# A two-layer sequence kernel on one core: the second layer's input slabs in a range of SBUF of their own, loads placed behind fetches of the last feed-forward, and three orders placed anew

## The chip, the core and the metric

One core of a Trainium2 chip runs the whole program. The metric is the device time of one execution in microseconds, as the median of several runs. TensorE (PE) does the matmuls, VectorE (DVE) and ScalarE (ACT) the elementwise work, GpSimd (POOL) small operations and the stores' DMA issues, SyncE (SP) most loads. All data are float32.

## The reference, cut to what matters

The input x is (4, 512, 128, 64): batch b, time t, features f, channels h. Layer 0:

```
xn = layernorm(x);  k, v = xn@Wk, xn@Wv;  r = sigmoid(xn@Wr)
s_t = decay*s_(t-1) + k_t*v_t;            x = x + (r*s) @ Wo
x = x + gelu(conv over f of layernorm(x))
x = x + layernorm(causal depthwise conv over t, 3 taps, of layernorm(x))
x = x + gelu(x @ ffn_W1 + b1) @ ffn_W2 + b2
```

Layer 1:

```
trend = moving_average(x, 25 steps of t);  seasonal = x - trend
xs = rfft(seasonal, over t)[:, :128]
out = trend + irfft(einsum('bmnc,cmk->bknc', xs, w_real + i*w_imag))
```

## The kernel before

Layer 0 handles each of the four sequences (b = 0 to 3) in stages: `project` (J: key, value and gate matmuls), `scan` (Z: the recurrence and a norm's moments), `attend_and_convolve` (A), `convolve_time` (C), `open_feed` (O: the first two units' input) and `feed_forward` (F). A unit is a pair of 128-row chunks by 512 time steps; `NPR` = 32 units make a sequence. Each stage is a Python generator that traces some work and yields a weight.

PE's order is written out: under `manual_schedule` PE's instructions run as traced, and `in_turn` walks two streams of stages side by side, a step of the one or of the other by how far each has come. The yield `CHAIN` (6.0) ends a step of a dependent chain, so that the other stream is stepped next:

```python
((0, (O, 0.05), (F, 0.95)), (2, (J, 0.88), (Z, 0.12))),
((1, (C, 1.0)), (2, (A, 1.0))),
((1, (O, 0.05), (F, 0.95)), (3, (J, 0.88), (Z, 0.12))),
((2, (C, 1.0)), (3, (A, 1.0))),
((2, (O, 0.05), (F, 0.95)), (3, (C, 0.95), (O, 0.05))),
((3, (F, 1.0)), (3, (nothing, 1.0))),
```

So sequence 3's feed-forward runs alone at the end of layer 0. The other engines and queues are ordered by a planner at compile time, which issues what is ready by its own estimate, in order of tracing where several are. Three calls bind it: `keep_in_program_order(i)` puts an instruction behind the one traced before it on its engine; `issue_after(i)` puts what is traced in its block, on the engine of i, behind i (the order only, no wait for the end of i). Waits for data and for a place in SBUF are added by the framework.

SBUF is given out in pools, one behind the other, and a pool that is opened later over the range of closed ones waits for them as a whole. Layer 0 has `decay` (2,048 bytes per partition), `fr` (tags `x1`, `z`, `xp`, `wx`, `wo`, `wcs`), `const`, `bk` and more; layer 1 begins again at the start with `dft` (2,048 bytes), `io` (tag `big`, five buffers of 8,192 bytes for slabs and mixing weights, and smaller tiles), `const1` and `spec` (the spectrum `xf`).

`wx` holds the projections' weights, the scan's `kv`, and in the last two feed-forwards the units' results, which DVE writes (L759) and PE transposes (L765) before they are copied to `ob` (L773, L778) and stored to `x4` in DRAM. In a feed-forward `residual` fetches `kx` and `kh` (L607) for the unit two ahead, DVE works on them (L692, L693, L704), PE makes `widen` (L733), ACT the activation `mid` (L738), and PE `narrow` (L746).

`project` for b > 1 loads weights for two units at a time and scales them on DVE (L358) before PE reads them (L408). The spread of a column over all rows (`spread`, L242) begins `rows`, whose input `rs` comes from POOL (L234) after DVE's copy of the moments (L269) and a few tiny operations (to L278).

Layer 1 loads a slab (512 time steps by 512 columns, 1 MB, three DMAs at L938 to L940) and `transform` makes `v`, `u` and `ev` of it on DVE (L959, L960, L963), `edge` copies on ACT (L956), and a group of two slabs' matmuls on PE (L971, L979, L988), copied to `xf` by ACT (L995). Sixteen groups make a pair of sequences. Then come `mix` (L1013, L1017) and `invert` (L1039 to L1073).

Of the kernel before, what the change touches and what calls it, by code (L numbers as in the profile page):

```python
# [1 line left out]

# [1 line left out]

# [6 lines left out]
F32 = mybir.dt.float32  # L11
AF = mybir.ActivationFunctionType
ALU = mybir.AluOpType
# [3 lines left out]
P = 128  # L17
# [28 lines left out]
@with_exitstack  # L46
def conv_seq_kernel(
    ctx: ExitStack,
    tc: tile.TileContext,
    x: bass.AP,  # L50
    xt: bass.AP,
    vecs: bass.AP,
    wkvr: bass.AP,
    wo: bass.AP,
    wdec: bass.AP,
    wconv: bass.AP,
    fbias: bass.AP,
    w1: bass.AP,
    fb1: bass.AP,
    w2: bass.AP,  # L60
    fb2: bass.AP,
    wri: bass.AP,
    dftv: bass.AP,
    dftd: bass.AP,
    dfte: bass.AP,
    idfte: bass.AP,
    idfto: bass.AP,
    avg: bass.AP,
    avgh: bass.AP,
    out: bass.AP,  # L70
):
    B = x.shape[0]
    dram = ctx.enter_context(tc.tile_pool(name="dram", bufs=1, space=DRAM))
    x4 = [dram.tile([T, D], F32, tag=f"x4_{b}", name=f"x4_{b}") for b in range(B)]

    layer0(tc, dram, x, xt, vecs, wkvr, wo, wdec, wconv, fbias, w1, fb1, w2, fb2, x4)
    layer1(tc, x4, wri, dftv, dftd, dfte, idfte, idfto, avg, avgh, out)


@with_exitstack  # L80
def layer0(ctx, tc, dram, x, xt, vecs, wkvr, wo, wdec, wconv, fbias, w1, fb1, w2, fb2, x4):
# [10 lines left out]

    decay = ctx.enter_context(tc.tile_pool(name="decay", bufs=1))
    fr = ctx.enter_context(tc.tile_pool(name="fr", bufs=3))
    const = ctx.enter_context(tc.tile_pool(name="const", bufs=1))
    bk = ctx.enter_context(tc.tile_pool(name="bk", bufs=2))
    rowp = ctx.enter_context(tc.tile_pool(name="rowp", bufs=1))
# [49 lines left out]
    nc.vector.tensor_copy(decb, dec.to_broadcast([P, T]))  # L147


    cgr = const.tile([P, NPR, H], F32, name="cgr")  # L150

    at_one = const.tile([P, 2], F32, name="at_one")
    nc.vector.tensor_reduce(at_one[:, 0:1], ident.rearrange("p (q k) -> p q k", k=32)[:, :, 1], mybir.AxisListType.X, ALU.add)
# [142 lines left out]
        return xp  # L296

    def spare(tag, n):
        return fr.tile([P, 2, n], F32, tag=tag, name=tag, bufs={"z": 4, "wx": 2}.get(tag, 3))

    def c_bank():
        return two(ps_c, "c")
# [17 lines left out]
    held = [False]  # L320
    narrowly = set()
    unscanned = [True]


    def project(b):
# [36 lines left out]
        ws, xps, xks = {}, {}, {}  # L362
        if b > 1:
            weights(0)
            for k in range(2):
                scale_weights(k, ws[k], True)
            xps[0] = load_x(b, 0)
        for i in range(NPR):
            first, last = i == 0, i == NPR - 1
# [51 lines left out]
    def scan(b):  # L421
# [13 lines left out]
        if b == 0:  # L435
# [25 lines left out]
            nc.vector.tensor_copy(qo[S:P, 0:S], pq[S:P, 0:S])  # L461
            nc.vector.tensor_scalar_mul(qo[S:P, S:], pq[S:P, S + 2 :], 1.0 / D)
        gw, bw, qo = sums["gw"], sums["bw"], sums["qo"]
        rb, mb = yield from rows(bank, rs, mean, "rm" if b > 1 else "rm3")
        if b == 0:
            kv = two(fr, "x1")
# [49 lines left out]
    def attend_and_convolve(b):  # L516
# [29 lines left out]
        def convolve(i):  # L546
            cv = c_bank() if i % 2 or held[0] else two(ps_m, "m")
            for h in range(2):
                for j in range(2):
                    q = 32 * (2 * h + j)  # L550
                    nc.tensor.matmul(
                        cv[h * H : (h + 1) * H, j, :], lhsT=cgr[q : q + 2, i, :], rhs=mb[q : q + 2, :],
                        start=True, stop=False,
                    )
            for j in range(2):
                c = 2 * i + j
                for n, h in neighbours(i % 2, c):
                    if 0 <= n < NCH:
                        rs = halves[rows_of(n // 2 % 2, n - c)]
                        nc.tensor.matmul(  # L560
                            cv[halves[h], j, :], lhsT=ws[n][rs, P:], rhs=zs[n][rs, :], start=False, stop=False
                        )
            for j in range(2):
                c = 2 * i + j
                nc.tensor.matmul(cv[:, j, :], lhsT=ws[c][:, 0:P], rhs=zs[c], start=False, stop=True)
            nc.scalar.activation(cv, cv, AF.Gelu_apprx_tanh)
            x2 = two(bk, "x2")
            nc.vector.tensor_tensor(x2, cv, x1s.pop(i), ALU.add)  # L568
            nc.gpsimd.dma_start(x2d[b][2 * i : 2 * i + 2].rearrange("c p t -> p c t"), x2)  # L569
            sq2 = bk.tile([P, 2, SL], F32, tag="sq", name="sq2")  # L570
            nc.scalar.activation(sq2, x2, AF.Square)  # L571
            for c in (2 * i - 2, 2 * i - 1):
                zs.pop(c, None)
                ws.pop(c, None)
            if i + 2 < NPR:
                scaled(i + 2)
            waiting[i] = x2, sq2
# [26 lines left out]

    def fetch(tag, src, b, i):
        t = bk.tile([P, 2, SL], F32, tag=tag, name=tag, bufs=3 if tag == "kx" else 2)
        nc.sync.dma_start(t, src[b][2 * i : 2 * i + 2].rearrange("c p t -> p c t"))  # L607
        return t


# [36 lines left out]
    def convolve_time(b):  # L647
        bank = of_a if b == B - 1 else of_p
        made = AHEAD if b in ahead else 0
        moment = carried.pop(b)  # L650
        if made:
            rb, mb = ahead.pop(b)
        else:
            rb, mb = yield from rows(bank, *moment, "rm" if b == B - 1 else "rm3")
        st = bank()
        waiting, added = [], 0
        n = NPR - made
        for k in range(n + 2):
            while waiting and waiting[0][0] == k - 2:
                add_up(st, 0, *waiting.pop(0)[1:], added == 0, added == NPR - 1)  # L660
                added += 1
            if k < n:
                if b == B - 1:

                    x2, xr, to, sq = spare("xp", SL), spare("x1", SL), spare("z", SL), two(bk, "sq")
                else:
                    x2 = bk.tile([P, 2, SL], F32, tag="kx", name="x2", bufs=3)
                    xr, to = two(bk, "kd"), bk.tile([P, 2, SL], F32, tag="k3", name="to", bufs=3)
                    sq = bk.tile([P, 2, SL], F32, tag="sq4", name="sq4", bufs=2)

                normed(b, made + k, x2, xr, rb, mb, made > 0 and k < 4)
                tapped(b, made + k, xr, to)
                nc.scalar.activation(sq, to, AF.Square)
                waiting.append((k, to, sq))
                i = k * made // n
                if i != (k + 1) * made // n:

                    to = fetch("kh", tod, b, i)
                    sq = bk.tile([P, 2, SL], F32, tag="mid", name="sq5", bufs=4)
                    nc.scalar.activation(sq, to, AF.Square)  # L680
                    waiting.append((k, to, sq))
            yield 7.0 * (NPR + 2) / (n + 2)
        mean, sq = yield from finish(st, bank, 4)
        causal[b] = moments(mean, sq, 4)


    def residual(b, i):
# [27 lines left out]
    def feed_forward(b):  # L715
# [69 lines left out]
        for i in range(NPR + lag):  # L785
            if i >= lag:
                store(i - lag)
            for q in range(4):
                done += quarter
                if i < NPR:  # L790
# [3 lines left out]
                        widen(i + 1, q - 2)  # L794
                    if i + 2 < NPR and q == 1:
                        coming = residual(b, i + 2)
                    if i + 2 < NPR and q == 3:
                        x3s[i + 2] = add_residual(b, i + 2, *coming)
                    narrow(i, q)
# [62 lines left out]
    with tc.manual_schedule(engines={nc.tensor.engine}):  # L862
        for _ in project(0):
# [10 lines left out]
            ((2, (O, 0.05), (F, 0.95)), (3, (C, 0.95), (O, 0.05))),  # L874
            ((3, (F, 1.0)), (3, (nothing, 1.0))),
        )


@with_exitstack
def layer1(ctx, tc, x4, wri, dftv, dftd, dfte, idfte, idfto, avg, avgh, out):  # L880

# [7 lines left out]
    G = 2  # L891

    dft = ctx.enter_context(tc.tile_pool(name="dft", bufs=1))
    io = ctx.enter_context(tc.tile_pool(name="io", bufs=2))
    const = ctx.enter_context(tc.tile_pool(name="const1", bufs=1))
    spec = ctx.enter_context(tc.tile_pool(name="spec", bufs=1))
# [29 lines left out]
            nc.vector.tensor_copy(dst, src)  # L926

    def slab(b, s):
        xin = io.tile([P, NT, SL], F32, tag="big", name="xin", bufs=5)
        nc.sync.dma_start(  # L930
            xin, x4[b][:, s * SL : (s + 1) * SL].rearrange("(c p) d -> p c d", p=P)
        )
        return xin

    def shifted_slab(b, s):
        xin = io.tile([P, NT, SL], F32, tag="big", name="xin", bufs=5)
        c = slice(s * SL, (s + 1) * SL)
        nc.sync.dma_start(xin[TURN:P, 0, :], x4[b][0 : P - TURN, c])  # L938
        nc.sync.dma_start(xin[0:TURN, 0, :], x4[b][T - TURN : T, c])
# [3 lines left out]
    def transform(b, xf):  # L943

        for g in range(NS // 2):
            edge = io.tile([P, SL], F32, tag="edge", name="edge")
            uv, ev, pf = [], [], []
            for k in range(2):
                s = 2 * g + k
                c = slice(s * SL, (s + 1) * SL)  # L950
                xin = shifted_slab(b, s)
                ends = xin[0 : 2 * TURN, 0, :]
                if k == 0:
                    first = ends
                for q in (32,) if k == 0 else (H, H + 32):
                    nc.scalar.copy(edge[q : q + 2 * TURN, :], ends)  # L956
                u = io.tile([P, 2, SL], F32, tag="uv0", name="u")
                v = io.tile([P, 2, SL], F32, tag="uv1", name="v")
                nc.vector.tensor_tensor(v, xin[:, 0:2, :], xin[:, 2:4, :], ALU.subtract)  # L959
                nc.vector.tensor_tensor(u, xin[:, 0:2, :], xin[:, 2:4, :], ALU.add)  # L960
                t = io.tile([P, 2, SL], F32, tag="ev", name="ev")
# [35 lines left out]
    def mix(xf):  # L997

        xc = xf.rearrange("p b r (a c l) -> p b r a c l", c=H, l=2)
        for g in range(H // CG):  # L1000

            w = io.tile([P, CG, 2, 2, M], F32, tag="big", name="w", bufs=5)
            nc.sync.dma_start(w, wri[:, g * CG : (g + 1) * CG, :, :, :])
            w4 = w[:, :, 1, 0, :].rearrange("p c (n i m) -> p c n i m", n=2, i=2)[:, :, :, 0, :]
            for t in (w4, w[:, :, 1, 1, 0:H]):
# [23 lines left out]
    def invert(b, xf):  # L1029
# [3 lines left out]
        def waves(s):  # L1033
# [12 lines left out]
            for i, op in enumerate((ALU.add, ALU.subtract)):  # L1046
                nc.vector.tensor_tensor(even[:, i, :], ev[0], two, op)
            for i in range(2):
                pm = io.tile([P, 2, SL], F32, tag=f"uv{i}", name="pm")
                for k, op in enumerate((ALU.add, ALU.subtract)):  # L1050
                    nc.vector.tensor_tensor(pm[:, k, :], even[:, i, :], od[i], op)
                halves[s].append(pm)
# [1 line left out]
        def trends(s):  # L1054
            c = slice(s * SL, (s + 1) * SL)
            xin = slab(b, s)
            halo = io.tile([P, SL], F32, tag="edge", name="halo")
            for j in range(NT):
                at = 32 * j
                if j > 0:  # L1060
# [137 lines left out]
```

## Time and profile before

| | us |
|---|---|
| median of 3 runs (lowest, highest) | 3731.04 (3726.51, 3733.54) |
| the profiled execution's own time | 3727.17 |
| its span | 3725.4 |
| PE busy | 3519.4 (94%) |
| DVE busy | 2671.6 (72%) |
| ACT busy | 1779.8 (48%) |
| last feed-forward of layer 0, first PE work to last | 2481.7 to 2743.9 |
| first pair's transform, to the first mixing matmul | 2743.9 to 2877.5 |
| second pair's transform, to its first mixing matmul | 3233.6 to 3358.7 |

Times in the profile are microseconds from the span's start. A timeline row has its start, the busy time of the merged instructions, engine, line, operation and names; in brackets stands the idle time of the engine before it and what ended it. `PE a L530 <- DVE x L532` in the table of waits says that the matmul of line 530 into `a` waited for DVE's instruction at line 532. SPq is SyncE's queue of DMA issues.

### The profile page before, as it was taken

To read this page: it belongs to the slowest core of one execution; us is meant where nothing else is said; L and a number is where in the kernel's file an instruction comes from. 1 tells how busy PE (TensorE), PEld (TensorE's weight loads), DVE (VectorE), ACT (ScalarE), POOL (GpSimd) and SP (SyncE) were. 2 spreads that over 40 slices of the span, in tenths; PEclk is the share of its full clock that TensorE was granted. 3 is DMA by queue.
4 is the path that set the end of the run, shared out by engine and by line. 5 is a ranking of instruction groups with operands and counts; after the bars stand their busy time and mean duration, and the time that the engine had idled before them with its cause. 6 is when DMAs were issued, how large, how long until landed. Compare 5 with 4: busy or idle time off the path is not lost. (4 is left out here: it accounts for less than half of the span.)

```text
span 3725.4 us, 53006 instructions
## 1 busy us (share of the span) xinstructions
PE 3519.4 (94%) x20041; PEld 1366.8 (37%) x20041; DVE 2671.6 (72%) x3498; ACT 1779.8 (48%) x2331; POOL 450.4 (12%) x654
## 2 busy tenths in 40 slices
PE   9999999989999999999999989899989999899998
PEld 4433322224333223433322333333323843328433
DVE  4455569976777896677789699946658277792677
ACT  0013346546666565566656588878855200152100
POOL 0000012220011211001122122100000000001000
PEclk9999999999999999999999999999999999999999
DMA  9867647777885787788478677645569479994687
GB/s 313 282 211 243 227 154 270 254 264 259 293 295 176 249 275 267 265 292 296 167 240 286 210 245 268 233 154 194 199 202 285 154 231 295 300 295 167 214 286 263
DMA packets 427223, 910.29 MB, mean 244 GB/s; under 512 B 32728, under 2 KB 83160, under 8 KB 422872
## 3 DMA queue, kind: packets, MB, share of 16 engines
q1 hardware_dynamic: 353136, 636.92, 52.7%
q0 software_dynamic: 71680, 268.46, 19.8%
q8 instruction: 160, 2.62, 0.3%
q10 hardware_dynamic: 2152, 1.51, 0.1%
q14 instruction: 95, 0.78, 0.1%
HBM read 638.26 MB, written 268.50 MB: 243 GB/s over the span
## 5 line engine op out<-in xcount | busy, mean ns | idle before, releaser
L746 PE MATMUL p<-mid,w_sb 64*64 64x512 f32 x2048 | 560.8, 595 | 24.0 <-DVE wx L759 23.3
L746 PE MATMUL pb<-mid,w_sb 64*64 64x512 f32 x2048 | 533.4, 595 | 0.0
L738 ACT ACTIVATE mid<-c,fb_sb 128x1024 f32<-128x1024 f32 x256 | 284.6, 1112 | 94.5 <-PE c L733 92.3
L738 ACT ACTIVATE mid<-m,fb_sb 128x1024 f32<-128x1024 f32 x256 | 285.0, 1113 | 91.2 <-PE m L733 89.7
L733 PE MATMUL c<-x,w_sb 64*64 64x512 f32 x2016 | 281.6, 606 | 11.1 <-ACT mid L738 7.0
L733 PE MATMUL m<-x,w_sb 64*64 64x512 f32 x2016 | 283.3, 609 | 5.6 <-ACT ob L778 3.4
L746 PEld LDWEIGHTS p<-mid,w_sb 64*64 64x64 f32 x2048 | 160.4, 134 | 289.6 <-issue 244.0
L408 PE MATMUL a<-xp,wx 128*128 128x512 f32 x512 | 240.0, 613 | 6.6 <-issue 6.6
L1044 ACT COPY two<-a 128x512 f32<-128x512 f32 x64 | 37.5, 587 | 428.4 <-PE a L1039 428.4
L1067 PE MATMUL b<-xin,avg_sb 128*128 128x512 f32 x512 | 230.8, 593 | 3.3 <-DVE xin L1073 3.3
L1073 DVE TENSOR_TENSOR xin<-b,pm 128x512 f32<-128x512 f32 x256 | 159.1, 684 | 99.2 <-PE b L1070 84.3
L571 ACT ACTIVATE sq<-x 128x1024 f32<-128x1024 f32 x128 | 135.2, 1056 | 181.4 <-DVE x L568 181.3
L626 DVE SCALAR_TENSOR_TENSOR to<-kd,vec,to 128x510 f32<-128x510 f32 (+1 forms) x272 | 197.7, 747 | 10.5 <-ACT to L622 9.4
L701 ACT ACTIVATE kd<-kd,vec 128x512 f32<-128x512 f32 x256 | 193.1, 805 | 3.3 <-DVE kd L693 3.3
L252 PE MATMUL st<-x,ones 128*32 128x512 f32 x512 | 174.2, 611 | 10.7 <-DVE x L568 10.6
L926 DVE COPY xf<-b 128x256 f32<-128x256 f32 x128 | 54.4, 425 | 178.9 <-PE b L1013 170.0
L626 DVE SCALAR_TENSOR_TENSOR z<-x,vec,z 128x511 f32<-128x511 f32 x240 | 176.2, 747 | 5.0 <-ACT z L622 3.6
L704 DVE TENSOR_TENSOR x<-kd,kx 128x1024 f32<-128x1024 f32 x126 | 154.2, 1224 | 33.8 <-ACT kd L701 33.8
L532 DVE TENSOR_TENSOR x<-a,xp 128x1024 f32<-128x1024 f32 x128 | 156.3, 1221 | 29.8 <-PE a L530 27.3
L530 PE MATMUL a<-rst,wo_sb 64*128 64x512 f32 x512 | 148.6, 654 | 27.4 <-DVE x L532 25.4
L759 DVE SCALAR_TENSOR_TENSOR x4t<-p,fb_sb,x 128x512 f32<-128x512 f32 x64 | 47.8, 747 | 159.8 <-PE pb L746 157.4
L569 POOL DMA_DIRECT2D x<-x x128 | 93.5, 731 | 566.7 <-DVE x L568 561.7
(269 smaller groups left out, 6830.1 us busy)
## 6 DMA issues: line engine op xcount, KB each, us to landing
xp<-in_xt SPq DMA_DIRECT2D x256, 512.0 KB
kh<-to SPq DMA_DIRECT2D x156, 512.0 KB
x<-x POOLq DMA_DIRECT2D x128, 512.0 KB, 4.6
kx<-x SPq DMA_DIRECT2D x128, 512.0 KB
x<-ob POOLq DMA_DIRECT2D x64, 1024.0 KB, 8.1
xin<-x SPq DMA_DIRECT2D x64, 1024.0 KB
out<-xin POOLq DMA_DIRECT2D x64, 1024.0 KB, 5.9
x<-x SPq DMA_DIRECT2D x96, 512.0 KB
```

Of the source, the lines that this page charges most:

```text
L252: nc.tensor.matmul(st[32 * q : 32 * q + 32, :], lhsT=ones, rhs=src[:, j, :], start=first, stop=last,)
L408: nc.tensor.matmul(pa[:, k, :], lhsT=wq[:, j, k * P : (k + 1) * P], rhs=xp[:, j, :], start=first and j == 0, stop=last and j == 1,)
L530: nc.tensor.matmul(at[:, j, :], lhsT=wo_sb[js, :], rhs=rst[js, :], start=True, stop=True)
L532: nc.vector.tensor_tensor(x1, at, xp, ALU.add)
L626: tap = nc.vector.scalar_tensor_tensor(to[:, j, k:], xr[:, j, : SL - k], vec[:, w, c], to[:, j, k:], ALU.mult, ALU.add)
L701: tc.keep_in_program_order(nc.scalar.activation(d[:, j, :], d[:, j, :], AF.Identity, bias=vec[:, B4, c], scale=vec[:, G4, c]))
L704: nc.vector.tensor_tensor(x3, d, x2, ALU.add)
L733: nc.tensor.matmul(pm[halves[j], h, :], lhsT=w1_sb[halves[h], q * H : (q + 1) * H], rhs=x3[halves[h], j, :], start=True, stop=True,)
L738: nc.scalar.activation(mid, pm, AF.Gelu_apprx_tanh, bias=fb1_sb[:, q : q + 1])
L746: nc.tensor.matmul(sums2[i][j][halves[h], :], lhsT=w2_sb[halves[j], q, :], rhs=mid[halves[j], h, :], start=q == 0, stop=q == 3,)
L1067: nc.tensor.matmul(po[j], lhsT=avg_sb[:, j, :], rhs=xin[:, j, :], start=True, stop=False)
L1073: nc.vector.tensor_tensor(by_n(xin[:, j, :]), by_n(po[j]), by_c(pm[j % 2][:, j // 2, :]), ALU.add)
```

## The change

- `wx` moves out of `fr` into a pool of its own, `wxp`, right behind `fr`; `cgr` moves from `const` into `fr`.
- Layer 1's slabs, mixing weights, `edge`, `halo`, `v` and one of the two `pm` tiles move from `io` into a new pool `slabs` ahead of it.
- Layer 0 gives back a list of its fetches of sequence 3's residuals (the last DMA of every fourth unit); the first five slabs of sequence 0 are queued on SyncE behind the third to the seventh of these.
- For b > 1 the scaling of the projection's first two units' weights is no longer pinned behind what DVE was given before it; it is queued behind the `x2` addition of the last but one unit of `attend_and_convolve` of the sequence before.
- A `CHAIN` yield is added in `scan` ahead of `rows` for b > 1, and one at the end of `convolve_time` for the last sequence.

```diff
+    wxp = ctx.enter_context(tc.tile_pool(name="wxp", bufs=2))
...
-    cgr = const.tile([P, NPR, H], F32, name="cgr")
+    cgr = fr.tile([P, NPR, H], F32, name="cgr", bufs=1)
...
     def spare(tag, n):
-        return fr.tile([P, 2, n], F32, tag=tag, name=tag, bufs={"z": 4, "wx": 2}.get(tag, 3))
+        if tag == "wx":
+            return wxp.tile([P, 2, n], F32, tag=tag, name=tag)
+        return fr.tile([P, 2, n], F32, tag=tag, name=tag, bufs=4 if tag == "z" else 3)
...
         if b > 1:
             weights(0)
-            for k in range(2):
-                scale_weights(k, ws[k], True)
+            with tc.issue_after(begin[project]):
+                for k in range(2):
+                    scale_weights(k, ws[k])
             xps[0] = load_x(b, 0)
...
         gw, bw, qo = sums["gw"], sums["bw"], sums["qo"]
+        if b > 1:
+            yield CHAIN
         rb, mb = yield from rows(bank, rs, mean, "rm" if b > 1 else "rm3")
...
-            nc.vector.tensor_tensor(x2, cv, x1s.pop(i), ALU.add)
+            whole_x2 = nc.vector.tensor_tensor(x2, cv, x1s.pop(i), ALU.add)
+            if i == NPR - 2:
+                begin[project] = whole_x2.ins
...
     def fetch(tag, src, b, i):
-        nc.sync.dma_start(t, src[b][2 * i : 2 * i + 2].rearrange("c p t -> p c t"))
+        last_fetch[0] = nc.sync.dma_start(t, src[b][2 * i : 2 * i + 2].rearrange("c p t -> p c t"))
...
         causal[b] = moments(mean, sq, 4)
+        if b == B - 1:
+            yield CHAIN
...
                     if i + 2 < NPR and q == 1:
                         coming = residual(b, i + 2)
+                        if b == B - 1 and i % 4 == 2:
+                            after.append(last_fetch[0].ins)
...
     dft = ctx.enter_context(tc.tile_pool(name="dft", bufs=1))
+    slabs = ctx.enter_context(tc.tile_pool(name="slabs", bufs=2))
     io = ctx.enter_context(tc.tile_pool(name="io", bufs=2))
...
-        xin = io.tile([P, NT, SL], F32, tag="big", name="xin", bufs=5)
+        xin = slabs.tile([P, NT, SL], F32, tag="big", name="xin", bufs=5)
...
-                xin = shifted_slab(b, s)
+                with tc.issue_after(after[s + 2]) if b == 0 and s < 5 else nullcontext():
+                    xin = shifted_slab(b, s)
...
-                v = io.tile([P, 2, SL], F32, tag="uv1", name="v")
+                v = slabs.tile([P, 2, SL], F32, tag="uv1", name="v")
```

More of the change, by code (lines that the diff above doesn't have):

```diff
@@ L1 @@
-from contextlib import ExitStack
+from contextlib import ExitStack, nullcontext
 import numpy as np
@@ L74, in conv_seq_kernel @@
     x4 = [dram.tile([T, D], F32, tag=f"x4_{b}", name=f"x4_{b}") for b in range(B)]
-    layer0(tc, dram, x, xt, vecs, wkvr, wo, wdec, wconv, fbias, w1, fb1, w2, fb2, x4)
-    layer1(tc, x4, wri, dftv, dftd, dfte, idfte, idfto, avg, avgh, out)
+    after = layer0(tc, dram, x, xt, vecs, wkvr, wo, wdec, wconv, fbias, w1, fb1, w2, fb2, x4)
+    layer1(tc, x4, wri, dftv, dftd, dfte, idfte, idfto, avg, avgh, out, after)
 @with_exitstack
@@ L322, in layer0 @@
     unscanned = [True]
+    last_fetch = [None]
+    after = []
     def project(b):
@@ L876, in layer0, with layer1 @@
         )
+    return after
 @with_exitstack
-def layer1(ctx, tc, x4, wri, dftv, dftd, dfte, idfte, idfto, avg, avgh, out):
+def layer1(ctx, tc, x4, wri, dftv, dftd, dfte, idfte, idfto, avg, avgh, out, after):
     nc = tc.nc
@@ L935, in shifted_slab @@
     def shifted_slab(b, s):
-        xin = io.tile([P, NT, SL], F32, tag="big", name="xin", bufs=5)
+        xin = slabs.tile([P, NT, SL], F32, tag="big", name="xin", bufs=5)
         c = slice(s * SL, (s + 1) * SL)
@@ L945, in transform @@
         for g in range(NS // 2):
-            edge = io.tile([P, SL], F32, tag="edge", name="edge")
+            edge = slabs.tile([P, SL], F32, tag="edge", name="edge")
             uv, ev, pf = [], [], []
@@ L1000, in mix @@
         for g in range(H // CG):
-            w = io.tile([P, CG, 2, 2, M], F32, tag="big", name="w", bufs=5)
+            w = slabs.tile([P, CG, 2, 2, M], F32, tag="big", name="w", bufs=5)
             nc.sync.dma_start(w, wri[:, g * CG : (g + 1) * CG, :, :, :])
@@ L1048, in waves @@
             for i in range(2):
-                pm = io.tile([P, 2, SL], F32, tag=f"uv{i}", name="pm")
+                pm = (slabs if i else io).tile([P, 2, SL], F32, tag=f"uv{i}", name="pm")
                 for k, op in enumerate((ALU.add, ALU.subtract)):
@@ L1056, in trends @@
             xin = slab(b, s)
-            halo = io.tile([P, SL], F32, tag="edge", name="halo")
+            halo = slabs.tile([P, SL], F32, tag="edge", name="halo")
             for j in range(NT):
```

## The prediction, made before the result was known

> **What bounds the kernel now.** I read the page first: TensorE (PE) is busy for 94% of the span, so only stretches where PE stands still can give much. Then PE's waits over the whole run, to find which few causes make up the idle time; then the busy times by stretch around the change from the first to the second layer; then the timelines of PE, VectorE (DVE) and of the SyncE DMA queue (SPq) at those places.
>
> ```profile
> span 3725.4 us, 53006 instructions
> PE p L746 <- DVE wx L759: 23.3, 7, 5.5
> PE a L971 <- DVE v L959: 20.4, 12, 9.4
> PE a L242 <- POOL rs L234: 12.3, 6, 4.0
> PE b L971 <- DVE v L959: 12.0, 15, 3.4
> PE a L408 <- issue: 6.6, 2, 4.1
> ```
>
> Columns: microseconds in total, times, longest. `v` at L959 is the first thing the second layer does with a slab of its input; `rs` at L234 ends a layer norm's short chain; L408 is the projection's first matmul.
>
> ```profile
> 2481.70:2743.90 262.20, 261.95 (x2305) 103.11 (x2304) 150.49 (x150) 211.96 (x237) 12.07 (x16) 1.00 0.50 171
> 2743.90:2753.30 9.40, 0.04 (x2) 0.07 (x3) 1.37 (x2) 1.69 (x3) 0.75 (x1) 0.61 0.82 256
> 2753.30:2819.40 66.10, 56.03 (x384) 14.57 (x384) 59.43 (x67) 33.03 (x58) 0.00 (x0) 0.98 1.00 296
> 2819.40:2877.50 58.10, 52.42 (x385) 15.30 (x385) 52.27 (x61) 30.77 (x55) 5.84 (x6) 1.00 0.97 304
> ```
>
> Stretch, length, busy time of PE, PE's weight loads, DVE, ACT, POOL, then granted clock, DMA share, GB/s. The last feed-forward (262 us) has PE full and DMA half idle. Then PE does nothing for 9.4 us, and the transform of the first pair takes until 2877.5 with the DMA engines full: 133.6 us in all. In its second half the groups follow each other every 6.95 us (L971 starts at 2819.4, 2826.4, 2833.3, 2840.3), which is DVE's own work for a group; in its first half every 7.2 to 8.7 us.
>
> ```profile
> 2705.82 0.36 SPq L607 DMA_DIRECT2D kx<-x  x1
> 2744.01 0.34 SPq L938 DMA_DIRECT2D xin<-x  x1
> SPq L938 <- PE c L765: 37.7, 1, 37.7
> 2753.26 3.37 PE L971 MATMUL a<-v,dftd_sb 128*64 128x512 f32 x8 [9.40 <-DVE v L959]
> ```
>
> SyncE's last fetch of the first layer goes at 2705.8; the first slab then waits 37.7 us for the last PE transposes (L765), which read `wx`. The slabs' data have long been in DRAM: it is the place in SBUF that is not free.
>
> ```profile
> 802.46 0.16 DVE L278 TENSOR_TENSOR mrs<-me,rs 128x4 f32<-128x4 f32 x1 [2.43 <-POOL rs L234]
> 802.54 1.92 DVE L358 TENSOR_SCALAR wx<-wx,vec 128x192 f32<-128x192 f32 x8
> 802.96 3.75 PE L408 MATMUL a<-xp,wx 128*128 128x512 f32 x4 [4.05 <-issue]
> 1145.35 1.16 PE L242 MATMUL a<-ident,rs 128*128 128x128 f32 x8 [1.91 <-POOL rs L234]
> 1797.60 1.16 PE L242 MATMUL a<-ident,rs 128*128 128x128 f32 x8 [1.63 <-POOL rs L234]
> 2456.76 2.08 PE L242 MATMUL a<-ident,rs 128*128 128x128 f32 x8 [4.04 <-POOL rs L234]
> ```
>
> The projection of sequence 2 waits at 798.9 for its scaled weights (L358), which stand in DVE's queue behind L278, which waits for POOL. Sequence 3 does the same at 1458.7 (2.58 us). The last three are chains with nothing put between.
>
> **The change, part by part.** No instruction is added or taken away; 15 slab DMAs (five slabs of three), eight weight scalings and the order of PE's stages move.
>
> *Slabs early.* Per partition, `fr` loses `wx` (12,288 B) and gains `cgr` (8,192 B): 55,296 B. The new pool `slabs` has 5 x 8,192 + 2 x 2,048 + 2 x 4,096 = 53,248 B and starts, behind equal 2,048 B, where `fr` starts. So it lies wholly over `fr`, whose last reader is DVE's L759 with `z` at 2499.7. The five anchors are fetches of units 12, 16, 20, 24 and 28; counting back from the last `kh` fetch (2698.95) by 8.15 us a unit, the slabs go out at about 2544, 2577, 2609, 2642 and 2674. They do not wait, and all have landed 60 us before they are used. On SPq 15 issues of about 0.4 us are put in front of later `kx`/`kh` fetches, 1.2 us per slab in a queue that waits most of a unit anyway. On POOL's queue nothing moves.
>
> Their bytes: 5.2 MB into a stretch at 171 GB/s. The Trainium skill ("Trainium Kernel Development and Optimization", Key Constraints) says that all queues share the same 16 DMA engines, which speaks against this: at the 304 GB/s of the full stretch a slab holds a fetch up by 3.5 us. By that rule alone five slabs cost up to 17 us; by the rows, DVE stands idle 2.7 us in each unit and a unit's input is used a whole unit (8.15 us) after its fetch. I take the rows: nothing on PE, 3.5 us each if that cover were gone.
>
> What the second layer's engines do: PE can start when the last copies out of PSUM end (2745.0). `v` of the first two slabs can be made before; `u` and `ev` are in the pool over `wx`, so DVE starts them at 2743.9. DVE then needs 16 groups x 6.95 = 111.2 us less two `v` (2.4): 2852.7, and from the last group's L979 to the first mixing matmul it is 4.65 us (2872.84 to 2877.49): 2857.4, a gain of 20.1. DMA: 27 slabs left, 28.3 MB at 304 GB/s = 93 us from about 2751, when the first group gives its slot back; last landing near 2846, so nearly tied with DVE. How soon one slab lands decides small stalls. The trace's chain has slabs at 7.3 to 9.5 us; the skill ("DMA: Bandwidth & Descriptors", Anatomy of one DMA) has 2 us plus bytes over 436 GB/s, 4.4 us for 1 MB, given for POOL's path. PE gives a group's first slot back 2.9 us after DVE is done with the group, and the slab that takes it is needed half-way through the second group after (6.95 + 3.4 us): 7.4 us of time, so no stall by the rule, up to 2 us at some groups by the rows. I take the rows: 7.1 us per group, 2.6 us lost, gain 17.5 (ends: 12 at 7.45 us per group, 22).
>
> Moved with the slabs: up to six `edge` copies of 0.62 us on ACT among the feed-forward's activations, where ACT waits 0.6 us for PE per quarter and PE follows closely. Cost 0 to 3.7; I take 1.5, as most of a copy fits a gap.
>
> *First weights.* With the scaling right behind the last-but-one `x2` add, PE waits only for DVE's copy that frees bank `a` (L269, ends 799.1 and 1458.9): 3.8 + 2.3 us gained. The four scalings fall into DVE idle times (2.2 us before L269; 3.7 us for sequence 3), so cost nothing; without these, 1 us each.
>
> *Two chains.* The extra yield after the projection (sequences 2 and 3) and after sequence 3's time convolution lets feed-forward units, which are waiting in turn, run on PE while POOL works: 1.9 + 1.6 + 4.0 = 7.5 us.
>
> *Clock.* After 4 us idle, the next rows are slow: L242 takes 2.08 us at 2456.8 against 1.16 at 2465.1, and in all some 2.9 us are lost there; L408 takes 3.75 for four at 803.0 against 1.98 at 1794.0, and twelve take 7.72 at 1461.2 against 5.40 right after: 4 us more. The skill ("TensorE: Matmul & The Clock Gate", What's actually happening) says that an idle window of about 3.4 us halves the clock. By it the 9.4 us gap at 2743.9 would be worth another 5 us or so; I give it nothing, because the transform waits for DVE at either clock. In the first layer I take 2.9 + 2, as part of the slowness has other gaps before it.
>
> *Given back.* Each later step of scans 2 and 3 now stands a seventh of 0.12 of a stage later, some 6 us of feed-forward, nearer to the DVE-full stretches; sequence 3's opening is also later by about 4 us against the end of feed-forward 2, whose last units wait for DVE already (2.35 us at 2472). I take 4 us of loss, from 0 to 10.
>
> Sum: 17.5 - 1.5 + 6.1 + 7.5 + 4.9 - 4 = 30.5, say 30 us. The profiled execution took 3727.2 us for its span of 3725.4; that becomes about 3697. The median shown is 3.9 us above the profiled execution, so 3701.
>
> **Rivals.** *The slabs do not come early* (a pool still waits as a whole for something late, or the queue sends them last). For it: the wait at L938 is for a whole pool today. Against it: the sizes above. Only the first layer's 13 to 14 us stay: 3717.
>
> *The orders give back what they save.* The new yields shift DVE work into stretches where it is full (59.5 of 60 us between 2160 and 2400). The first layer then gives nothing, the slabs 16: 3715.
>
> *ACT is held up by slabs (slower).* ACT's queue is in order. If `edge` copies of slabs 0 to 3 are queued right behind the slabs' issue, ACT stands for a landing (up to 9.5 us) four times in a feed-forward that needs it every 1.7 us: about 7 us of PE each, plus 2.9 us of slow clock as after 2452, 40 us together, against 30 gained: 3741. It decides from 7.5 us per slab. Against it: an `edge` copy reads only the first 256 KB of a slab, and the feed-forward's own activations are ready first.
>
> **How the numbers follow.** Working out: 0.74, 3701, by its bounds 3689 to 3713. Slabs late: 0.07. Orders give back: 0.10. ACT held up: 0.09, of which a little lies near no change. A measurement of this kernel can tell about 0.2% (7.5 us). Faster by more: 0.86; within: 0.06; slower: 0.08. The range to hold it 8 in 10 takes in both milder rivals: 3689 to 3718.
>
> **What would show it.** Right: five `xin` loads at L938 to L940 between 2540 and 2680; the first L971 within 2 us of the last L765; stage from there to L1013 near 115 us instead of 133.6; the L408 waits near 0.3 us; no 4 us wait at L242 before the last opening. Wrong: a first `xin` only after the last transpose; new waits of PE on `mid` (L738) in the last feed-forward; groups at 7.5 us or more, or longer waits on `wx` and L530 at the ends of feed-forwards 0 to 2.

## The result: slower, by the mechanism of the third rival

| | before | changed |
|---|---|---|
| median, us | 3728.82 (4 runs, 3726.51 to 3733.54) | 3752.93 (4 runs, 3742.99 to 3756.59) |
| ratio of times, with 95% interval | 1 | 1.006 (1.0042 to 1.0079) |
| profiled execution, its span | 3727.17, 3725.4 | 3742.99, 3741.2 |
| last feed-forward, first PE work to last transpose | 261.9 | 303.7 |
| from there to the first mixing matmul | 133.9 | 116.7 |

The forecast was 3701, with 3689 to 3718 as its range. The profiled execution of the changed kernel is the fastest of its four; the sums below are made in it (15.8 us over before), and the median is a further 8 us up. The last two rows of the table, and all stretches below, are counted to the start of the last transpose; the times before the prediction go to its end, 0.3 us later.

Line numbers have moved: L745/L750/L758 are widen, `mid` and narrow (L733/L738/L746 before), L771 and L777 are the unit's sum into `wx` and its transpose (L759, L765), L954 to L956 load a slab, L973 is the edge copy (L956 before), L976 is `v` (L959), L988 the transform's first matmul (L971), L243 the spread. The page's first line and PE's table of waits after the change:

```profile
span 3741.2 us, 52994 instructions
PE m L777 <- ACT mid L750: 40.6, 6, 8.1
PE p L758 <- DVE wx L771: 17.7, 6, 5.7
PE a L988 <- DVE v L976: 10.4, 12, 3.7
PE a L243 <- POOL rs L235: 8.9, 5, 3.4
```

A wait that wasn't there before heads the list: a transpose into bank `m` that waits for an activation. The wait on `v` that the change was after has fallen from 20.4 to 10.4 us for bank `a`. The same two stretches as before, by engine:

```profile
2474.80:2778.50 303.70, 271.94 (x2305) 107.34 (x2304) 154.80 (x154) 215.30 (x242) 12.07 (x16) 0.94 0.50 168
2778.50:2895.20 116.70, 106.27 (x772) 30.20 (x770) 109.58 (x126) 62.08 (x109) 7.24 (x7) 1.00 0.96 295
```

The second row is the forecast gain: 17.2 us off the boundary (17.5 was forecast), and no 9.4 us of dead time at its head. The first row is the loss: PE stands for 31.8 of 303.7 us and its granted clock is 0.94 instead of 1.00, in a stretch that had no idle PE before. The timelines at the first of four such places (start, duration, what; in brackets the wait before it). SPq, which issues the slab's three loads:

```profile
2539.01 1.39 SPq L954 DMA_DIRECT2D xin<-x  x1
2540.45 1.08 SPq L955 DMA_DIRECT2D xin<-x  x1
2541.59 0.42 SPq L956 DMA_DIRECT2D xin<-x  x1
```

ACT, with the edge copy between two `mid`:

```profile
2537.98 1.11 ACT L750 ACTIVATE mid<-c,fb_sb 128x1024 f32<-128x1024 f32 x1 [0.25 <-PE c L745]
2548.01 0.62 ACT L973 COPY edge<-xin 32x512 f32<-32x512 f32 x1 [8.92 <-DMA xin<-x]
2548.65 1.11 ACT L750 ACTIVATE mid<-m,fb_sb 128x1024 f32<-128x1024 f32 x1
```

DVE, with `v` in front of a sum:

```profile
2549.77 1.23 DVE L976 TENSOR_TENSOR v<-xin 128x1024 f32<-128x1024 f32 x1 [10.24 <-DMA xin<-x]
2550.91 0.75 DVE L771 SCALAR_TENSOR_TENSOR wx<-p,fb_sb,x 128x512 f32<-128x512 f32 x1
```

And PE:

```profile
2549.82 1.97 PE L777 MATMUL m<-ident,wx 128*128 128x128 f32 x8 [7.68 <-ACT mid L750]
```

The loads go out where they should. But the planner has put the edge copy of this slab on ACT as the next instruction after their issue, in front of two `mid` activations whose matmuls are long done, and `v` on DVE in front of the next sum. Each of the two engines takes its queue in order: ACT stands for 8.9 us, DVE for 10.2, until what they need of the slab has landed. PE has two banks for widen, fills both, and stops at 2542.1. The transpose, when it comes, takes 1.97 us (the granted clock is 0.50 from 2548 to 2552) instead of 1.09.

### The profile page after: what moved, and what is told of

Its sections match the earlier page's. It is cut to its first block, busy times and chain, and to the rows that moved or that the text cites. A ratio compares the mean times of both kernels' runs of the same rounds, so it can differ in the third digit from the quotient of the medians.

```text
span 3741.2 us, 52994 instructions
## 1 busy us (share of the span) xinstructions
PE 3523.6 (94%) x20041; PEld 1363.7 (36%) x20041; DVE 2668.9 (71%) x3498; ACT 1778.2 (48%) x2331; POOL 449.1 (12%) x654
## 5 line engine op out<-in xcount | busy, mean ns | idle before, releaser
L758 PE MATMUL p<-mid,w_sb 64*64 64x512 f32 x2048 | 555.4, 601 | 17.7 <-DVE wx L771 17.7
L758 PE MATMUL pb<-mid,w_sb 64*64 64x512 f32 x2048 | 538.4, 600 | 0.0
L750 ACT ACTIVATE mid<-m,fb_sb 128x1024 f32<-128x1024 f32 x256 | 284.9, 1113 | 92.5 <-PE m L745 91.0
L750 ACT ACTIVATE mid<-c,fb_sb 128x1024 f32<-128x1024 f32 x256 | 284.5, 1111 | 91.9 <-PE c L745 91.1
L745 PE MATMUL c<-x,w_sb 64*64 64x512 f32 x2016 | 283.7, 616 | 13.2 <-ACT mid L750 6.9
L745 PE MATMUL m<-x,w_sb 64*64 64x512 f32 x2016 | 283.2, 613 | 7.4 <-ACT ob L790 5.2
L758 PEld LDWEIGHTS p<-mid,w_sb 64*64 64x64 f32 x2048 | 154.5, 136 | 299.7 <-issue 269.0
L771 DVE SCALAR_TENSOR_TENSOR x4t<-p,fb_sb,x 128x512 f32<-128x512 f32 x64 | 47.8, 746 | 172.0 <-PE pb L758 171.9
```

What stands on the lines that cost most here:

```text
L745: nc.tensor.matmul(pm[halves[j], h, :], lhsT=w1_sb[halves[h], q * H : (q + 1) * H], rhs=x3[halves[h], j, :], start=True, stop=True,)
L750: nc.scalar.activation(mid, pm, AF.Gelu_apprx_tanh, bias=fb1_sb[:, q : q + 1])
L758: nc.tensor.matmul(sums2[i][j][halves[h], :], lhsT=w2_sb[halves[j], q, :], rhs=mid[halves[j], h, :], start=q == 0, stop=q == 3,)
```

## Experiments

### 1. Hold the edge copies, hold v, hold both

In the first kernel the edge copies of the first five slabs are queued on ACT behind the last copy into `ob`; in the second, `v` on DVE behind the last sum; in the third, both. Nothing else of the change is touched; the lines that only pass the two anchors on (`copied`, `summed`) are left out of the cuts.

```diff
-                for q in (32,) if k == 0 else (H, H + 32):
-                    nc.scalar.copy(edge[q : q + 2 * TURN, :], ends)
+                with tc.issue_after(copied) if b == 0 and s < 5 else nullcontext():
+                    for q in (32,) if k == 0 else (H, H + 32):
+                        nc.scalar.copy(edge[q : q + 2 * TURN, :], ends)
```

```diff
-                nc.vector.tensor_tensor(v, xin[:, 0:2, :], xin[:, 2:4, :], ALU.subtract)
+                with tc.issue_after(summed) if b == 0 and s < 5 else nullcontext():
+                    nc.vector.tensor_tensor(v, xin[:, 0:2, :], xin[:, 2:4, :], ALU.subtract)
```

Edge copies held:

> The changed kernel, with the edge copies of the first five slabs queued on ACT behind the last copy into ob. Theory ACT (ACT's in-order queue stands still for four slabs' landings): the four waits of 7.7 to 8.1 us of PE at the transposes go, the last feed-forward is back from 298.7 to about 263 us, the span falls from 3741 to about 3703 (31.8 us of waits and some 5 us of slow clock), faster than the kernel before. Rival DVE (the subtraction v, queued early on DVE, holds the units' sums up): two of the four waits stay, about 3722. Rival traffic (the slabs' bytes hold kx and kh up): all four stay, about 3741.

v held:

> The changed kernel, with v of the first five slabs queued on DVE behind the last sum of the last feed-forward; the edge copies stay as they are. Theory ACT: the four waits of about 8 us stay, the span stays within 3 us of 3741. Rival DVE: two of the four waits go, about 3722. Rival traffic: about 3741 as well.

Both held:

> The changed kernel with both held: nothing of the second layer but the five slabs' loads stands in the last feed-forward. Theory ACT: as with the edge copies alone held, about 3703, within 2 us. Rival DVE: a further 18 us less than with the edge copies alone held. Rival traffic: waits at kx and kh stay and the last feed-forward stays over 290 us.

| | median, us | ratio to before (95%) | last feed-forward | PE's waits over 1 us in it |
|---|---|---|---|---|
| changed | 3752.9 | 1.006 (1.0042 to 1.0079) | 303.7 | four, 7.7 to 8.1 |
| edge held | 3733.6 | 1.0014 (1.0002 to 1.0025) | 283.2 | two, 7.3 and 7.4 |
| v held | 3755.9 | 1.0078 (1.0056 to 1.0099) | 304.0 | four, 7.7 to 8.3 |
| both held | 3711.7 | 0.9955 (0.9943 to 0.9968) | 263.1 | none |

PE's longest waits in the last feed-forward, in the kernel with edge held:

```profile
PE p L759 <- DVE wx L772: 14.7, 2, 7.4
```

PE's and ACT's, in the one with `v` held:

```profile
PE m L778 <- ACT mid L751: 32.2, 4, 8.3
ACT edge L974 <- DMA xin<-x: 36.0, 4, 9.5
```

(The changed kernel's last feed-forward, 298.7 us in the first expectation, is 303.7 in the trace.) The theory said that with the edge copies held all four waits go, and the rival on DVE said two stay. Neither was whole. All four waits on `mid` go, and two of another name come up, of narrow on the sum (L772), which stands behind `v` in DVE's queue (timeline, edge held):

```profile
2553.86 1.23 DVE L978 TENSOR_TENSOR v<-xin 128x1024 f32<-128x1024 f32 x1 [10.00 <-DMA xin<-x]
2555.00 0.75 DVE L772 SCALAR_TENSOR_TENSOR wx<-p,fb_sb,x 128x512 f32<-128x512 f32 x1
```

Two, since `v` has two buffers; four on ACT, since `edge` has two buffers of two slabs each. Holding `v` alone frees nothing, as the same landings stop ACT. So two queues waited for the same landings, and either of them stops PE; only with both held are all waits gone. A stall's price: (283.2 - 263.1) / 2 = 10.1 us with DVE's two, (303.7 - 263.1) / 4 = 10.2 us with ACT's four, of which some 8 us are idle and 2 to 3 us are slow clock after it. The rival on traffic is out: with both held the five loads still run in the feed-forward, which takes 263.1 us against 261.9, and the 1.2 us over come before the first of them. In the two kernels of experiment 5, which have the loads but not the yield before the last opening, it takes 261.8, as before. The row of the one with the slabs' part alone (the DMA engines move 192 GB/s where it was 171):

```profile
2496.10:2757.90 261.80, 261.59 (x2304) 103.03 (x2304) 150.88 (x151) 211.71 (x236) 12.05 (x16) 1.00 0.57 192
```

What the yield does there: PE waits at the last transposes of sequence 2's feed-forward, and so begins the last one at a low clock. Rows of PE just before it in the changed kernel, and its first:

```profile
2468.36 1.09 PE L777 MATMUL m<-ident,wx 128*128 128x128 f32 x8
2472.87 1.97 PE L777 MATMUL c<-ident,wx 128*128 128x128 f32 x8 [3.42 <-DVE wx L771]
2474.76 1.99 PE L745 MATMUL m<-z,w_sb 64*64 64x512 f32 x8
```

### 2. How long is a stall?

The five loads go behind fetches of the units one earlier, in which no 1 MB store of `ob` runs; edge and `v` stand free, as in the changed kernel.

```diff
-                        if b == B - 1 and i % 4 == 2:
+                        if b == B - 1 and i % 4 == 1:
```

> The changed kernel with the five slabs' loads behind the fetches of the units one earlier (9, 13, 17, 21, 25), in which no 1 MB store of ob runs beside them; edge and v are not held. Theory landing (each stall is as long as the slab takes to land, and that takes 9 us because a store, kh and the slab share the DMA engines): the four waits of about 8 us shrink to some 5 us each, the last feed-forward from 304 to about 290 us, the span to about 3730. Rival (the stall has a fixed length, by the order alone): four waits of 7.5 to 8.2 us stay, about 3741.

3740.4 us, ratio 1.0053 (1.003 to 1.0075). The four waits are 4.5, 5.8, 5.3 and 5.8 us, and the feed-forward takes 294.5 us:

```profile
PE c L777 <- ACT mid L750: 21.4, 4, 5.8
```

So a stall follows the landing: without the store beside it, a slab's first edge copy starts 5.8 to 6.8 us after its first load's issue, where it was 8.9 to 9.7. The landing theory's 5 us and 290 us were a little low, and its 3730 by 8 us of the profiled span.

### 3. Leave the yields in the scans out

Both held, and without the yield in `scan`.

```diff
-        if b > 1:
-            yield CHAIN
         rb, mb = yield from rows(bank, rs, mean, "rm" if b > 1 else "rm3")
```

> As the one with both held, without the two added yields in the scan of sequences 2 and 3. Theory yields (they cost 6.4 and 5.4 us between the end of the projection and the next stage, by a sigmoid that waits on ACT ahead of the feed-forward's activations, and a chain with nothing left to put between): another 10 to 12 us less, about 3692. The prediction's own step (the yields gain 3.5 us, less up to 4 given back): no change or 4 us more.

3696.1 us, ratio 0.992 (0.9888 to 0.9951), 15.6 us under both held by medians. From the last projection matmul to the last widen of the feed-forward beside it:

| | sequence 2 | sequence 3 |
|---|---|---|
| before | 66.8 | 66.7 |
| changed | 73.3 | 72.2 |
| both held | 72.3 | 71.4 |
| both held, no scan yields | 66.8 | 66.5 |

The yields cost 5 to 6 us each there, where the prediction had them gain 1.9 and 1.6. The three other kernels without them (experiments 5 and 6) take 68.4 to 68.9 in sequence 2 and 66.5 to 66.9 in sequence 3, so in sequence 2 the cost may be nearer 4 us. The rest of the 15.6 us is not settled: from that widen to sequence 3's first projection matmul this kernel and that of experiment 4 take 245.4 us, all others 248.4 to 252.2, and nothing that these experiments edit stands in that stretch.

### 4. Count the scan as eight steps

Why do they cost? The stages' progress is reckoned as a yield's weight over `whole`, in which the scan counts as seven steps and now has eight. Both held, with the yields, and the count mended:

```diff
-        J: 2.0 * NPR, Z: 7 * CHAIN, A: 7.0 * NPR + 3 * CHAIN, C: 7.0 * (NPR + 2) + 3 * CHAIN, O: 4 * CHAIN,
+        J: 2.0 * NPR, Z: 8 * CHAIN, A: 7.0 * NPR + 3 * CHAIN, C: 7.0 * (NPR + 2) + 3 * CHAIN, O: 4 * CHAIN,
```

> As the one with both held, with the scans' added yields, but with the scan counted as eight steps and not seven where the streams' progress is reckoned. Theory cover (seven eighths of the steps fill the share, so the last steps run with nothing between): the wait of 2.1 us at the next stage's spread goes, some 5 of the 15 us come back, about 3707. Theory sigmoid (ACT's queue stands 4.2 us at the sigmoid): that wait stays and with it most of the loss, about 3711. If both hold, each takes its part.

3695.2 us, ratio 0.9918 (0.9885 to 0.995); 66.8 and 67.3 us in the table's terms (68.5 and 68.4 in the second kernel of experiment 6, which counts the scan in the same way). PE's waits in sequence 2's stretch, in the changed kernel:

```profile
PE m L777 <- ACT mid L750: 4.4, 1, 4.4
PE c L777 <- DVE x4t L771: 2.5, 2, 1.5
PE a L243 <- POOL rs L235: 2.1, 1, 2.1
```

And in this one:

```profile
PE c L779 <- DVE x4t L773: 5.8, 3, 3.3
PE m L779 <- DVE x4t L773: 2.9, 3, 1.0
```

Both waits go, the sigmoid's and the spread's, not the one that theory cover named alone. In the changed kernel the sigmoid stands 4.2 us at the head of ACT's queue, in front of a `mid`; with the steps spaced out it waits 1.9 us and PE loses nothing by it. The loss came from the reckoning: counted rightly, the same yields cost between nothing and 2 us. How, the program says: seven steps fill the share, so the eighth and the next stage's first follow with nothing between; and every step lies otherwise against the feed-forward, which the runs don't tell apart from it. The yields still gain nothing: the wait of 1.9 us on `rs` is away, but those at the transposes have grown from 5.3 us before to 8.7, the longest from 2.3 to 3.3.

### 5. Parts alone

Only the slabs' part, both held, with first weights and both chains as before:

```diff
-            with tc.issue_after(begin[project]):
-                for k in range(2):
-                    scale_weights(k, ws[k])
+            for k in range(2):
+                scale_weights(k, ws[k], True)
...
-        if b > 1:
-            yield CHAIN
...
-        if b == B - 1:
-            yield CHAIN
```

> Of the change only the slabs' part (ranges and early loads), with edge and v held to the end of the last feed-forward; the first weights and both chains are as in the kernel before. Theory (early loads give the gain, at the boundary): the first layer stays within 4 us of before, the stretch from the last transpose to the first mixing matmul is 119 to 122 us instead of 133.9, the span about 3711. Rival (the ranges of SBUF themselves or the loads' bytes cost something in the first layer): over 3717.

3710.0 us, ratio 0.996 (0.9948 to 0.9971), by which it is 15 us (11 to 19) faster than before. The boundary takes 118.6 us, just under the 119 to 122 expected. Its profiled execution is the longest of its 20 runs (its span is 3725.8): it is 11 us late already at the last matmul of sequence 1's convolution. That matmul stands between 780.9 and 798.1 us in the profiled executions of the kernels here, though nothing of the change but places in SBUF comes before it; so parts are read by their own stretches, and totals by medians.

Experiment 3's kernel without the yield before the last opening too, so without any added yield, but with the first weights' part:

```diff
         causal[b] = moments(mean, sq, 4)
-        if b == B - 1:
-            yield CHAIN
```

> As the one with both held and no yields in the scans, and without the yield at the end of the last time convolution too. Theory (that yield saves a 4.0 us wait and 2.9 us of slow clock): the wait of about 4 us at the spread before the last opening is back, 6 to 8 us more than with it, about 3703. Rival (the yield only moves the wait to the last units of the feed-forward): within 2 us of it, about 3696.

3705.0 us, ratio 0.9938 (0.992 to 0.9957), against 0.992 (0.9888 to 0.9951) with that yield: the intervals overlap, so the stretch has to decide. From the first widen of feed-forward 2 to that of feed-forward 3 it takes 358.0 us, against 350.5 with the yield and 357.8 before. The last feed-forward then takes 261.8 us against 263.0 with the yield, which gives 1.2 of the 7.5 us back: the rival, by which the wait only moves to the last units, is right for that part. The wait is back in this kernel (PE's timeline):

```profile
2452.38 2.08 PE L243 MATMUL a<-ident,rs 128*128 128x128 f32 x8 [4.04 <-POOL rs L235]
```

In the changed one the same matmul starts with no wait and at full clock:

```profile
2458.12 1.16 PE L243 MATMUL a<-ident,rs 128*128 128x128 f32 x8
```

### 6. Edge and v after the landing, inside the feed-forward

Instead of the feed-forward's end, the anchors are its own activation and sum of the unit traced three units behind the loads' fetch; no scan yields. (As fetches run ahead of the units, this is not 24 us, as the expectation has it: the first edge copy starts 54 us after its slab's first load.)

```diff
+                    if b == B - 1 and i % 4 == 1 and i > 4 and q == 3:
+                        landed.append((last_mid[0].ins, last_sum[0].ins))
...
+                with tc.issue_after(landed[s + 2][0]) if b == 0 and s < 5 else nullcontext():
```

> As the one with both held and no yields in the scans, but the edge copies and v of a slab are queued three units (24 us) behind its loads, inside the last feed-forward. Theory (the stall is the wait for the landing, not the copies' own time): the slabs have landed, no wait of PE over 1 us appears in the last feed-forward, it stays within 2 us of 263 us, and the transform's start gains about 2 us, since v and edge are made before: 3690 to 3696. Rival (ACT has no room for the copies): the feed-forward grows by 4 us or more, about 3699.

3699.2 us, ratio 0.9924 (0.9902 to 0.9946), not faster than holding to the end (0.992). There is no stall: the wait was for the landing. But the feed-forward is 266.4 us and the boundary 118.0, against 263.0 and 120.9: the 3.4 us more in the feed-forward are close to the copies' own time on ACT (six of 0.62 us, 3.7 us); that the transform gives them back is not shown, as boundaries differ by more from kernel to kernel (below).

Then only `v` there, edge held to the end, and the scan counted as eight:

> As the one with both held and the scan counted as eight, but v of the first two slabs is made in the last feed-forward, three units behind the loads; the edge copies stay held to its end. Theory (DVE has room there, 2.7 us idle per unit, ACT has not): the feed-forward stays within 1.5 us of 263 us, and the stretch to the first mixing matmul is 1 to 3 us shorter than 119.8: about 3694. Rival (DMA sets the transform's pace anyway): no shorter, within 1 us of it.

3690.3 us (3687.4 to 3690.9), ratio 0.9913 (0.9896 to 0.993). It has the lowest median here, but by its ratio it can't be told from the two kernels at 0.992. The two stretches:

```profile
2460.40:2723.80 263.40, 263.21 (x2305) 103.47 (x2304) 154.75 (x154) 211.60 (x236) 12.06 (x16) 0.99 0.58 194
2723.80:2841.80 118.00, 106.23 (x772) 30.16 (x769) 109.73 (x126) 65.72 (x115) 6.96 (x7) 1.00 0.96 292
```

DVE takes the two `v` with the feed-forward at 263.4, and the boundary is 1.8 us shorter than the 119.8 of the one with both held to the end. Boundaries of the kernels here lie between 116.3 and 121.1, and not in the order of what was made early, so that gain is within their spread.

## Why the prediction was wrong

| step, us | forecast | measured in the profiled executions |
|---|---|---|
| slabs early, boundary | -17.5 | -17.2 |
| edge copies and `v` in the last feed-forward | +1.5 | +40.6 |
| first weights, with clock | -6.1, -2 | -2.9 and -3.0 |
| yields in the scans | -3.5, and 4 given back | +6.5 and +5.5 |
| yield before the last opening, with clock | -4.0, -2.9 | -7.2, +1.2 |

The 40.6 is the changed kernel's last feed-forward less that with both held (303.7 - 263.1). The measured column sums to 23.5, where this profiled execution is 15.8 over before: it was 6.5 ahead at the end of sequence 1's convolution, the stretch in which executions differ most (experiment 5), lost 0.7 between the scan and the next projection, and gained 1.9 behind the first mixing.

*The step that failed* is "Moved with the slabs": it priced the copies' own time on ACT, 0 to 3.7 us, of which it took 1.5, and `v` at nothing; measured were 40.6. A moved instruction also brings its wait into the queue in front of all that comes after, and the price of that is the landing. The prediction had worked this out, as its slower rival: four stalls, 40 us, 3741. Four stalls of 40.6 us in all came. Its total, 3741 against a median of 3752.9, was too low by about the 12 us that the scans' yields lost. What it got wrong was the chance, 0.09, and both reasons against it. "The feed-forward's own activations are ready first" was an assumption on the planner's order, which the trace of before could not show; the planner put the copy right behind the issue. "Reads only the first 256 KB": the copy started 1.8 us ahead of `v`, which needs the whole slab, so it bought almost nothing. And the rival named ACT alone; DVE had the same fault (experiment 1).

*A smaller failure* is "Two chains" for the scans: the wait of 1.9 us was put down as gain without the reckoning of `whole`, where the scan stands as a constant of seven. The step "Given back" saw the shift by a seventh and sized the loss at 4 us from 0 to 10; it was about 12 (experiments 3 and 4).

*First weights* were mis-sized: L408's wait went (4.05 to 0.3 us), but eight scalings (the four of the first two units, and four that follow them in the program) were put in front of the last `x2` of sequence 1, and PE's wait on it grew from 1.8 to 3.8 us, before and after:

```profile
793.43 1.87 PE L252 MATMUL st<-x,ones 128*32 128x512 f32 x2 [1.80 <-DVE x L568]
788.95 1.86 PE L253 MATMUL st<-x,ones 128*32 128x512 f32 x2 [3.82 <-DVE x L576]
```

They were not hidden, as the prediction had it; 1 us was its price without that cover, and it had counted four.

*What held.* The boundary, the pools' ranges, the loads' times (2546.7 to 2676.8 with both held, for 2544 to 2674), and no cost by traffic on PE (the row, not the rule of shared engines, decided rightly: 261.8 us against 261.9). That the boundary came within 0.3 us is in part luck, as it differs by 5 us from kernel to kernel (and the 2.6 us set off for slower groups are 2.4 by the prediction's own figures, 16 times 7.1 less 6.95). The yield before the last opening gained 6.0 us for the 6.9 forecast, by other terms: a wait of 4.0 us at the spread and one of 2.3 on `wx` went, one of 3.4 at the last transposes came, and the rest, some 3 us, goes with the clock. With the two faults out (both held, no scan yields) the kernel takes 3696 us; the sum had forecast 3701. That its profiled execution is 30.7 us under that of before, against the 30.5 of the sum, is luck: its boundary gained 13.0 and not 17.5, and 3.8 us came from the unsettled stretch of experiment 3, up to sequence 2's last convolution matmul.

## What to carry to other kernels

A load moved early is harmless only if what reads it stays late, on every engine: the planner here queued the readers right behind the issue, and in an in-order queue each stands until its data have landed. So give each moved load two anchors, one for the load and one for its first readers, and look for readers on all engines, since the second culprit hides behind the first. When a step is added to a schedule that reckons in shares, its total has to be raised with it.

## What the runs showed of the hardware that was not expected

A 224 KB and a 32 KB load, issued at 2539.0 and 2540.5, were not usable until 2548.0 while a 1 MB store, 0.5 MB of `kh` and the slab's other 768 KB moved beside them: the DMA engines moved 298 to 411 GB/s from 2540 to 2548. The small part of the slab was usable hardly before the whole (1.8 us).

The same 5.2 MB cost PE nothing where nothing waited for them at once: 261.8 us of feed-forward with them, 261.9 without.

A stall of 7.3 to 8.3 us of PE costs about 10 us, since PE runs at a granted clock of 0.50 for a while behind it; the shorter ones of 4.5 to 5.8 us cost (294.5 - 263.1) / 4 = 7.9 us each.
